# Transposing on TensorE in place of a round trip through DRAM, in the last five of 64 graphs

## The chip, the cores and the metric

The kernel runs on one core of a Trainium2 chip. The metric is the device time of one execution in microseconds (us). The names of the engines in the profile are PE (TensorE, matrix products and transposes by product), PEld (its loading of weights), DVE (VectorE), ACT (ScalarE), POOL (GpSimd) and SP (SyncE, which issues most transfers).

## The reference, cut to what matters

Each of 64 independent graphs has 256 nodes with 256 features (`x`) and a 256 x 256 integer adjacency (`adj`). Four layers follow each other, each with a residual and a layer norm around it:

```python
def _layernorm(x, axis=-1, eps=1e-5): ...           # no scale, no shift
x = _layernorm(x + _L0_gnn_ref(x, adj, ...))        # 8-head masked attention and a feed-forward of 1024
x = _layernorm(x + _L1_gnn_ref(x, adj, ...))        # graph attention (GAT)
x = _layernorm(x + _L2_gnn_ref(x, adj, ...))        # graph attention, then elu
x = _layernorm(x + _L3_gnn_ref(x, adj, ...))        # two relational convolutions, each with elu

# a graph attention (layers 1 and 2)
hidden = x @ W                                      # 256 x 256
e = leaky_relu(f_i[:, None] + f_j[None, :], 0.2)    # f_i, f_j: hidden times two vectors
out = softmax(where(adj > 0, e, -big)) @ hidden

# a convolution (twice in layer 3); with these inputs one of the two relations is empty
out = x @ w_root + b
for r in range(R):
    out = out + (einsum('ij,id->jd', masks[r], x) / deg[r]) @ w_rel[r]
h = elu(out)
```

Everything is in 32-bit floating point. [...] the input `x` of `x @ W`, which lies with nodes on partitions, must first be turned so that features lie on partitions. This happens five times in each graph after the projections: once ahead of the feed-forward, and once ahead of each of the two graph attentions and the two convolutions.

## The kernel before

A planner records every operation of every graph with a cost, and a list scheduler then fixes the order in which each engine executes them. Several graphs are in flight at a time. The last five graphs (`LAST = 5`) have due times close together, so that they are worked on side by side. Buffers come from rings; the numbers are their sizes:

```python
RINGS = {..., "T": 4, ..., "turned": 1, "xT": 2}
DRAM = {"rows": 6}
...
plan.ring("bank", 8, bank)               # PSUM: eight banks

class Plan:
    PERIOD = 46.0
    LAST, SPACE = 5, 0.1
    def schedule(self):
        last = max(o.graph for o in self.ops) - self.LAST
        for i, o in reversed(list(enumerate(self.ops))):
            due = (min(o.graph, last) + self.SPACE * max(0, o.graph - last)) * self.PERIOD
            ...
```

There are two ways to turn a tile `xt` of 256 nodes by 256 features. The first is used ahead of the feed-forward: four transposes on TensorE into one PSUM bank, and one copy out of it on ScalarE.

```python
def transposed(xt):
    xT, pt = new("T", [P, KB, N]), new("bank", [P, KB, N])
    def issue():
        for kb in range(KB):
            for i in range(NB):
                nc.tensor.transpose(pt()[:, kb, i * P : (i + 1) * P], xt()[:, i, kb * P : (kb + 1) * P], ident)
    pe("full", 0.44, issue, [xt], [pt], [xT])
    act(0.47, lambda: nc.scalar.copy(xT(), pt()), [pt], [xT])
    return xT
```

The second, called a bounce here, is used ahead of graph attentions and convolutions. VectorE transposes blocks of 32 x 32 into `turned`, four transfers store it in DRAM (`rows`), and one transfer loads it back with the blocks in place:

```python
def bounced(xt):
    turned, rows, xT = new("turned", [P, 4, NB * KB, 32]), new("rows", [P, NB * KB, 4, 32]), new("T", [P, NB * KB, P])
    dve(0.63, lambda: nc.vector.transpose(turned()..., xt()...), [xt], [turned], "uses")
    for a in range(4):
        op("SP", 0.5, lambda a=a: nc.sync.dma_start(rows()...[:, :, a, :], turned()[32 * a : 32 * a + 32]...),
           [turned], [(rows, a)], lag=SENT)
    op("SP", 0.5, lambda: nc.sync.dma_start(xT()..., rows()...), [rows], [xT], lag=BACK)
    return xT, lambda kb, i: xT()[:, KB * i + kb, :]
```

A bounce puts the features of a group of 128 on the partitions in another order: feature 32 b + c lies on partition 4 c + b. The rows of the weights of graph attentions and convolutions are loaded in that order once, at the start (`spread`), so that the product is the same.

The two users, cut to the steps that follow each other. A graph attention:

```python
def gat(xt, layer, gm, seen, bias, finish):
    xT, xT_at = bounced(xt)
    ...
    # per half: product with w (PE), copy of the result to h (ACT or DVE)
    # spread of one column over the partitions (PE), e = min(. + ., gm) (DVE), leaky relu (DVE), exp (ACT)
    # per half: product of e with h (PE), reciprocal and residual (DVE, in layer 2 also an exp on ACT)
    # then layer_norm: statistics (DVE), root (POOL), apply (ACT)
```

A convolution:

```python
def conv(h, layer, rel, rdeg):
    hT, hT_at = bounced(h)
    # per half: product with w, 512 columns (PE), hi = rounded part (ACT), lo = rest (DVE), o = . + bias (DVE)
    # per half: gather by rel (PE), o = o + . * rdeg (DVE)
    act(0.52, lambda: nc.scalar.activation(n(), o(), AF.Exp), [o], [n])
    act(0.52, lambda: nc.scalar.activation(n(), n(), AF.Identity, bias=minus[:, 0:1]), [n], [n])
    dve(0.60, lambda: nc.vector.scalar_tensor_tensor(o(), n(), 0.0, o(), op0=ALU.min, op1=ALU.max), [n, o], [o], "uses")
    return o
```

Of the kernel before, what the change touches and what calls it, by code (L numbers as in the profile page):

```python
# [17 lines left out]
P = 128  # L18
# [2 lines left out]
BIG = 1e30  # L21
NO_EDGE = -346.0


SENT, BACK = 3.0, 4.5

# [186 lines left out]
def tile_gnn_stack(ctx: ExitStack, tc: tile.TileContext, t: dict, out: bass.AP):  # L213
# [16 lines left out]
    nc = tc.nc  # L230
    x_in, adj_in = t["x"], t["adj"]
    B, N, D = x_in.shape
    assert N == 2 * P and D == 2 * P and B % 2 == 0
    G = B // 2
    KB = D // P
# [250 lines left out]
    def main_path(plan):  # L486
# [86 lines left out]
        def graph(g):  # L573
# [9 lines left out]
            def act(cost, issue, reads, writes):  # L583
                op("ACT", cost, issue, reads, writes)
# [4 lines left out]
            def tok(ring, dtype=F32):  # L589
                return new(ring, [P, NB, D], dtype)  # L590
# [20 lines left out]
            def transposed(xt):  # L611
# [9 lines left out]
                act(0.47, lambda: nc.scalar.copy(xT(), pt()), [pt], [xT])  # L621
                return xT

            def bounced(xt):

                turned, rows, xT = new("turned", [P, 4, NB * KB, 32]), new("rows", [P, NB * KB, 4, 32]), new("T", [P, NB * KB, P])
                dve(0.63, lambda: nc.vector.transpose(turned().rearrange("p b q n -> p (b q n)"),  # L629
                                                      xt().rearrange("p i (k b c) -> p b (i k) c", k=KB, b=4)),  # L630
                    [xt], [turned], "uses")
                for a in range(4):
                    op("SP", 0.5, lambda a=a: nc.sync.dma_start(  # L633
                        rows().rearrange("(c b) q a n -> c (b q) a n", b=4)[:, :, a, :],
                        turned()[32 * a : 32 * a + 32].rearrange("c b q n -> c (b q) n")), [turned], [(rows, a)], lag=SENT)
                op("SP", 0.5, lambda: nc.sync.dma_start(xT().rearrange("p q n -> p (q n)"), rows().rearrange("p q a n -> p (q a n)")),
                   [rows], [xT], lag=BACK)
                return xT, lambda kb, i: xT()[:, KB * i + kb, :]
# [178 lines left out]
                return y  # L817

            def gat(xt, layer, gm, seen, bias, finish):
                xT, xT_at = bounced(xt)  # L820
                w, c_w = gw[layer], c_gw[layer]
                h, e, z = new("h", [P, NB, HW]), tok("e"), tok("X")
                for i in range(NB):
                    ph = new("bank", [P, D + 2])
                    pe("full", 0.87, lambda i=i, ph=ph: product(ph(), lambda kb: xT_at(kb, i),
                                                                lambda kb: w[:, kb, :], KB), [xT, c_w], [ph], [h])
                    if bias is None:
                        act(0.27, lambda i=i, ph=ph: nc.scalar.copy(h()[:, i, 0 : D + 2], ph()), [ph], [(h, i)])
                    else:
                        dve(0.34, lambda i=i, ph=ph: nc.vector.tensor_tensor(h()[:, i, 0 : D + 2], ph(), bias, op=ALU.add),  # L830
                            [ph], [(h, i)])
                dve(0.07, lambda: nc.vector.memset(h()[:, :, ONE : ONE + 1], 1.0), [(h, 0), (h, 1)], [(h, "one")])
                dve(0.07, lambda: nc.vector.tensor_tensor(seen_fg[:, seen], h()[:, :, F_COL : G_COL + 1],
                                                          h()[:, :, F_COL : G_COL + 1], op=ALU.mult), [(h, 0), (h, 1)], [], "uses")
                pf = new("bank", [P, N])

                def spread():
                    for i in range(NB):
                        nc.tensor.transpose(pf()[:, i * P : (i + 1) * P],  # L839
                                            h()[:, i, F_COL : F_COL + 1].to_broadcast([P, P]), ident)  # L840

                pe("full", 0.22, spread, [(h, 0), (h, 1)], [pf], [e])
                for i in range(NB):
                    dve(0.40, lambda i=i: nc.vector.scalar_tensor_tensor(e()[:, i, :], pf(), h()[:, i, G_COL : G_COL + 1],  # L844
                                                                         gm()[:, i, :], op0=ALU.add, op1=ALU.min),
                        [pf, (h, i), gm], [(e, i)])
                dve(0.60, lambda: nc.vector.scalar_tensor_tensor(e(), e(), SLOPE, e(), op0=ALU.mult, op1=ALU.max), [e], [e],
                    "uses")
                act(0.52, lambda: nc.scalar.activation(e(), e(), AF.Exp), [e], [e])  # L849
                for i in range(NB):  # L850
                    po, r = new("bank", [P, HW]), new("r", [P, 1])
                    pe("full", 0.87, lambda i=i, po=po: product(po(), lambda kt: e()[:, kt, i * P : (i + 1) * P],
                                                                lambda kt: h()[:, kt, :], NB), [e, h], [po], [z, r])
                    dve(0.08, lambda po=po, r=r: nc.vector.reciprocal(r(), po()[:, ONE : ONE + 1]), [po], [r])
                    finish(i, z, po, r)
                return z
# [37 lines left out]
            def conv(h, layer, rel, rdeg):  # L894

                w, c_w, bias = conv_w[layer], c_cw[layer], conv_b[layer]
                hT, hT_at = bounced(h)
                o, hi, lo, n = tok("o"), new("hi", [P, NB, D + 2], F32R), tok("lo", F32R), tok("e")  # L900
                cols = D if layer else D + 2
                for i in range(NB):
                    po = new("bank", [P, 2 * D])
                    pe("full", 1.72, lambda i=i, po=po: product(po(), lambda kb: hT_at(kb, i),
                                                                lambda kb: w[:, kb, :], KB), [hT, c_w], [po], [hi, lo, o])
                    act(0.27, lambda i=i, po=po: nc.scalar.copy(hi()[:, i, 0:D], po()[:, D:]), [po], [(hi, i)])  # L906
                    dve(0.34, lambda i=i, po=po: nc.vector.tensor_tensor(
                        lo()[:, i, :], po()[:, D:], hi()[:, i, 0:D].bitcast(F32), op=ALU.subtract), [po, (hi, i)], [(lo, i)])
                    dve(0.33, lambda i=i, po=po: nc.vector.tensor_tensor(o()[:, i, :], po()[:, 0:D], bias, op=ALU.add),
                        [po], [(o, i)])  # L910
                if layer == 0:
                    dve(0.07, lambda: nc.vector.memset(hi()[:, :, D:].bitcast(F32), 1.0), [(hi, 0), (hi, 1)], [(hi, "ones")])
                for j in range(NB):
                    pa = new("bank", [P, D + 2])
                    terms = [(0, hi, cols), (0, lo, D), (1, lo, D), (1, hi, cols)]

                    def gather(j=j, pa=pa):
                        for c, (i, part, n) in enumerate(terms):
                            nc.tensor.matmul(pa()[:, 0:n], lhsT=rel()[:, i, j * P : (j + 1) * P], rhs=part()[:, i, 0:n],  # L919
                                             start=(c == 0), stop=(c == len(terms) - 1))  # L920

                    pe("full", 0.48, gather, [rel, hi, lo], [pa])
                    if layer == 0:
                        def inverse(j=j, pa=pa):
                            nc.vector.tensor_scalar(rdeg()[:, j : j + 1], pa()[:, D : D + 1], 1.0, None, op0=ALU.max)
                            nc.vector.reciprocal(rdeg()[:, j : j + 1], rdeg()[:, j : j + 1])

                        dve(0.25, inverse, [pa], [(rdeg, j)])
                    dve(0.40, lambda j=j, pa=pa: nc.vector.scalar_tensor_tensor(  # L929
                        o()[:, j, :], pa()[:, 0:D], rdeg()[:, j : j + 1], o()[:, j, :], op0=ALU.mult, op1=ALU.add),  # L930
                        [pa, (rdeg, j), (o, j)], [(o, j)])

                act(0.52, lambda: nc.scalar.activation(n(), o(), AF.Exp), [o], [n])
                act(0.52, lambda: nc.scalar.activation(n(), n(), AF.Identity, bias=minus[:, 0:1]), [n], [n])
                dve(0.60, lambda: nc.vector.scalar_tensor_tensor(o(), n(), 0.0, o(), op0=ALU.min, op1=ALU.max),
                    [n, o], [o], "uses")
                return o

            xT = input_transposed()
            adj = load("adj", adj_graph[g], I32)  # L940
            am, gm = masks(adj)
            xt = load("x", x_graph[g], F32)
# [4 lines left out]
            xt = feed_forward(x1, load("xr", x_graph[g], F32))  # L947
            xt = layer1(xt, gm)
            xt = layer2(xt, gm)
            rel = relation(load("adj", adj_graph[g], I32))  # L950
            rdeg = new("rdeg", [P, NB])
            h = conv(conv(xt, 0, rel, rdeg), 1, rel, rdeg)
# [270 lines left out]
```

## Time and profile before

The time is 2896.01 us, the median of three runs (2893.25 to 2898.55). The profiled execution has a span of 2897.1 us with a mean granted TensorE clock of 0.991. What matters in it:

| | |
|---|---|
| bounces in the program | 256 (four in each of 64 graphs) |
| VectorE block transposes for them (`turned<-X`, `turned<-o`) | 192 and 64 instructions, 134.9 and 45.0 us busy |
| stores into `rows` | 1024 of 64 KB, 2.2 us to landing |
| loads out of `rows` | 256 of 256 KB, 2.8 us to landing |
| transposes on TensorE ahead of the feed-forward (`bank<-ident,X`) | 256, 39.9 us busy |
| copies of those out of their bank on ScalarE (`T<-bank`) | 64, 37.5 us busy |

The page of a profile gives the busy time of each engine, then the span in 40 equal slices with a digit for each (9 means 90% busy or more), the transfers, and the chain of work that ended last, followed back from the last instruction. A row of a group of instructions names line, engine, operation, what is written and read, their shapes and count, then the busy time and the mean duration in ns of one, then the idle time of the engine just ahead of them and what ended it. A busy engine on its own says little: what a change is worth in a stretch of time is read from what the next operation of that stretch waited for.

### The profile page before, as it was taken

The page shows a single profiled execution, that of the slowest core. Times are in us where ns is not written, and L with a number is a line of the kernel's source. Part 1 is how long each engine was busy: PE and PEld are TensorE (multiplying, and loading weights), DVE is VectorE, ACT ScalarE, POOL GpSimd, SP SyncE. Part 2 cuts the span into 40 slices and gives each one's busy share as a digit, 9 for nine tenths or more (in the row PEclk, how much of TensorE's full clock was granted, in tenths as well). Part 3 has the DMA queues.
Part 4 walks back from the last instruction along what each step waited for, and adds up shares of the span by engine and source line. Part 5 has one row for each costly group of instructions (what it writes and reads, how often), then busy time and mean ns, then how long its engine had stood idle before and what let it go on. Part 6 is the DMA issues. An engine that isn't in the chain of part 4 may idle for free.

```text
span 2897.1 us, 50588 instructions
## 1 busy us (share of the span) xinstructions
PE 2805.3 (97%) x16182; PEld 2128.1 (73%) x16182; DVE 2523.0 (87%) x6557; ACT 1540.4 (53%) x3713; POOL 789.1 (27%) x1685
## 2 busy tenths in 40 slices
PE   8999999999999999999999999999999999999975
PEld 6776777777777767777777777777777777777853
DVE  6879899989989898999889898899888998999686
ACT  3555555546455555655555465555555655555343
POOL 2232223222223222222222322232231332222221
PEclk9999999999999999999999999999999999999998
DMA  7454455445444444454444544444444544443342
GB/s 183 81 108 88 99 101 102 89 101 102 95 92 100 87 94 94 98 101 93 104 97 93 98 99 99 100 91 102 86 93 96 109 88 93 105 90 72 67 83 70
DMA packets 844512, 278.32 MB, mean 96 GB/s; under 512 B 692656, under 2 KB 810672, under 8 KB 844240
## 3 DMA queue, kind: packets, MB, share of 16 engines
q1 hardware_dynamic: 808800, 240.27, 37.7%
q0 software_dynamic: 35440, 34.76, 8.5%
q8 instruction: 131, 2.15, 0.3%
q14 instruction: 141, 1.16, 0.1%
HBM read 157.43 MB, written 83.89 MB: 83 GB/s over the span
## 4 chain that ended last, share of the span: by engine, by line
PE 82%; DVE 10%; ACT 3%; DMA 2%; issue 2%; POOL 1%; SPq 1%; DVEq 0%; POOLq 0%; ACTq 0%
PE bank L657 67%; PE bank L919 4%; PE bank L776 3%; PE bank L751 3%; PE bank L771 2%; DMA rows<-turned 2%; DVE p L759 1%; PE bank L618 1%; DVE turned L629 1%; PE bank L839 1%; SPq L633 1%; DVE st L666 1%; DVE o L929 1%; DVE both L763 1%; DVE e L844 1%
## 5 line engine op out<-in xcount | busy, mean ns | idle before, releaser
L671 POOL TENSOR_SCALAR rstd<-mv 128x2 f32<-128x2 f32 x384 | 104.4, 272 | 1869.8 <-DVE mv L668 1496.7
L678 ACT ACTIVATE X<-X,rstd 128x256 f32<-128x256 f32 x640 | 349.8, 597 | 244.7 <-POOL rstd L674 230.1
L657 PE MATMUL bank<-cw,T 128*128 128x512 f32 x1024 | 467.9, 600 | 9.6 <-DMA T<-rows 9.1
L657 PE MATMUL bank<-T,w 128*128 128x256 f32 x2048 | 471.6, 380 | 5.2 <-ACT p L757 2.6
L657 PE MATMUL bank<-w,hid 128*128 128x256 f32 x2048 | 460.1, 380 | 0.0
L657 PEld LDWEIGHTS bank<-w,hid 128*128 128x128 f32 x2048 | 385.9, 190 | 62.7 <-issue 10.4
L657 PEld LDWEIGHTS bank<-T,w 128*128 128x128 f32 x2048 | 382.7, 190 | 64.5 <-issue 6.9
L757 ACT ACTIVATE p<-bank 128x512 f32<-128x512 f32 x512 | 299.9, 598 | 87.8 <-PE bank L751 87.6
L657 PEld LDWEIGHTS bank<-cw,T 128*128 128x128 f32 x1024 | 192.2, 192 | 209.3 <-issue 195.2
L759 DVE TENSOR_TENSOR p<-p,am 128x512 f32<-128x512 f32 x512 | 332.8, 680 | 10.8 <-ACT p L757 10.7
L672 POOL TENSOR_TENSOR rstd<-rstd,neghalf 128x2 f32<-128x2 f32 x384 | 305.7, 796 | 32.1
L809 ACT ACTIVATE hid<-bank,col_b 128x256 f32<-128x256 f32 x512 | 209.4, 474 | 113.8 <-PE bank L657 112.1
L657 PE MATMUL bank<-xT,wqkv 128*128 128x256 f32 x1024 | 251.6, 387 | 13.4 <-DVE xT L650 12.9
L657 PE MATMUL bank<-h,e 128*128 128x259 f32 x1024 | 253.8, 388 | 11.0 <-ACT e L849 9.3
L657 PE MATMUL bank<-gw,T 128*128 128x258 f32 x1024 | 249.1, 384 | 2.1 <-ACT inv L783 1.5
L657 PEld LDWEIGHTS bank<-h,e 128*128 128x128 f32 x1024 | 192.7, 192 | 66.6 <-issue 19.3
L666 DVE BATCH_NORM_STATS2 st<-X 128x6 f32<-128x256 f32 x640 | 237.5, 413 | 1.8
L906 ACT CAST hi<-bank 128x256 fp32r<-128x256 f32 x256 | 94.6, 370 | 263.4 <-PE bank L657 262.6
L657 PEld LDWEIGHTS bank<-xT,wqkv 128*128 128x128 f32 x1024 | 189.7, 192 | 54.0 <-issue 13.5
L780 DVE RECIPROCAL inv<-bank 128x256 f32<-128x256 f32 x128 | 220.0, 1734 | 8.8 <-PE bank L776 8.6
L657 PEld LDWEIGHTS bank<-gw,T 128*128 128x128 f32 x1024 | 191.1, 191 | 36.7 <-issue 5.2
L629 DVE STREAM_TRANSPOSE turned<-X 128x512 f32<-128x512 f32 x192 | 134.9, 703 | 45.0 <-DMA rows<-turned 23.0
(121 smaller groups left out, 4775.4 us busy)
## 6 DMA issues: line engine op xcount, KB each, us to landing
rows<-turned SPq DMA_DIRECT2D x1024, 64.0 KB, 2.2
T<-rows SPq DMA_DIRECT2D x256, 256.0 KB, 2.8
adj<-in_adj_dram SPq DMA_DIRECT2D x128, 256.0 KB, 3.0
blocks<-in_x_dram SPq DMA_DIRECT2D x512, 32.0 KB, 2.3
x<-in_x_dram SPq DMA_DIRECT2D x64, 256.0 KB, 3.0
xr<-in_x_dram SPq DMA_DIRECT2D x64, 256.0 KB, 2.8
xr<-row_ln_b POOLq DMA_DIRECT2D x64, 256.0 KB, 4.4
x<-row_bo POOLq DMA_DIRECT2D x64, 256.0 KB, 4.8
```

What stands on the lines that cost most here:

```text
L629: dve(0.63, lambda: nc.vector.transpose(turned().rearrange("p b q n -> p (b q n)"), xt().rearrange("p i (k b c) -> p b (i k) c", k=KB, b=4 ...
L657: nc.tensor.matmul(dst, lhsT=lhs(c), rhs=rhs(c), start=(c == 0), stop=(c == n - 1))
L666: nc.vector.bn_stats(stat()[:, i, :], y()[:, i, :])
L671: nc.gpsimd.tensor_scalar(rstd()[:, 0, :], mv()[:, :, 1], 1.0, EPS, op0=ALU.mult, op1=ALU.add)
L672: nc.gpsimd.tensor_tensor(rstd()[:, 0, :], rstd()[:, 0, :], neghalf[:, 0:NB], op=ALU.pow)
L678: nc.scalar.activation(y()[:, i, :], y()[:, i, :], AF.Identity, bias=rstd()[:, 1, i : i + 1], scale=rstd()[:, 0, i : i + 1])
L757: act(0.58, lambda pr=pr, k=k, sr=s[r]: nc.scalar.activation(pr(), sr(), AF.Exp, accum_out=seen_sum[:, k : k + 1]), [s[r]], [pr])
L759: dve(0.60, lambda pr=pr, kt=kt: nc.vector.tensor_tensor(pr(), pr(), am()[:, kt, None, :].to_broadcast([P, KB, N]), op=ALU.mult), [pr, am] ...
L780: dve(1.62, lambda hg=hg, pc=pc: nc.vector.reciprocal(inv()[:, hg, :], pc()[:, 1, :]), [pc], [(inv, hg)])
L809: act(0.36, lambda f=f, k=k, ph=ph: nc.scalar.activation(hid()[:, f + k, :], ph()[:, k, :], AF.Relu, bias=b1[:, f + k : f + k + 1]), [ph, ...
L906: act(0.27, lambda i=i, po=po: nc.scalar.copy(hi()[:, i, 0:D], po()[:, D:]), [po], [(hi, i)])
L919: nc.tensor.matmul(pa()[:, 0:n], lhsT=rel()[:, i, j * P : (j + 1) * P], rhs=part()[:, i, 0:n], start=(c == 0), stop=(c == len(terms) - 1))
```

## The change: TensorE transposes behind a spreading copy

In the last five graphs the four bounces of each graph are replaced by the first way, with a copy on ScalarE ahead of it. The copy writes the features of each group of 128 in the order in which the weights' rows lie (feature 32 b + c to column 4 c + b), so the transposed tile has on its partitions what a bounce would have put there, and the weights stay as they are. The purpose is to shorten the way from a tile to its transpose at the end of the program. In the other 59 graphs bounces stay. The copy's buffer comes from the same ring, `turned`, that has one buffer.

```diff
+QUICK = 5
...
+            def rearranged(xt):
+
+                if g < B - QUICK:
+                    return bounced(xt)
+                spread = tok("turned")
+                act(0.8, lambda: nc.scalar.copy(spread().rearrange("p i (k c b) -> p (i k) c b", k=KB, b=4),
+                                                xt().rearrange("p i (k b c) -> p (i k) c b", k=KB, b=4)), [xt], [spread])
+                xT = transposed(spread)
+                return xT, lambda kb, i: xT()[:, kb, i * P : (i + 1) * P]
+
             def bounced(xt):
...
             def gat(xt, layer, gm, seen, bias, finish):
-                xT, xT_at = bounced(xt)
+                xT, xT_at = rearranged(xt)
...
-                hT, hT_at = bounced(h)
+                hT, hT_at = rearranged(h)
```

## The prediction

> **What bounds the kernel now.** I read the page first: the engine totals and the 40 slices. TensorE has work for nearly all of the span, and only the first slice and the last two are not full.
>
> ```profile
> PE 2805.3 (97%) x16182; PEld 2128.1 (73%) x16182; DVE 2523.0 (87%) x6557; ACT 1540.4 (53%) x3713; POOL 789.1 (27%) x1685
> PE   8999999999999999999999999999999999999975
> ```
>
> The reader should take from it a ceiling: 2897.1 - 2805.3 = 91.8 us of TensorE idle in all, and the change acts only in the last five of 64 graphs, that is at the right-hand end of the second line. So I next asked for the busy time by stretches over that end.
>
> ```profile
> 2725.00:2737.00 12.00, 12.00 (x59) 10.48 (x58) 7.86 (x24) 5.72 (x13) 3.71 (x12) 1.00 0.16 44
> 2737.00:2760.00 23.00, 17.86 (x81) 14.20 (x79) 18.52 (x63) 7.77 (x16) 9.08 (x22) 1.00 0.51 91
> 2760.00:2800.00 40.00, 31.79 (x116) 22.88 (x117) 31.27 (x102) 17.58 (x38) 7.40 (x20) 0.87 0.38 76
> 2800.00:2830.00 30.00, 24.77 (x91) 14.58 (x90) 25.11 (x80) 12.38 (x26) 4.13 (x12) 1.00 0.45 91
> 2830.00:2860.00 30.00, 21.58 (x64) 11.05 (x63) 23.00 (x70) 11.96 (x25) 4.69 (x12) 0.89 0.43 94
> 2860.00:2884.80 24.80, 15.92 (x49) 7.95 (x47) 13.61 (x39) 8.26 (x16) 2.57 (x8) 0.86 0.22 59
> 2884.80:2897.10 12.30, 0.19 (x2) 0.09 (x2) 2.98 (x9) 2.45 (x4) 1.28 (x4) 0.61 0.09 27
> ```
>
> The columns are the stretch, its length, then busy time of PE, weight loads, DVE, ACT and POOL with their instructions, the granted clock, the DMA share and GB/s. TensorE is full until 2737. From there to its last matmul at 2884.8 it works 17.86 + 31.79 + 24.77 + 21.58 + 15.92 = 111.9 of 147.8 us, so **35.9 us are idle**. The last 12.3 us are the end of the last layer norm and the output's transfer, where TensorE has nothing to do. Up to 2737 there is no free TensorE time to win by a shorter wait.
>
> In the tail no engine is full: VectorE, summed likewise, works 111.5 of the 147.8 us and ScalarE 58.0. So work there is bound by the chain from one operation to the next. I looked at the DMA queue's timeline and the chain that ended last:
>
> ```profile
> 2808.95 2.56 SPq L633 DMA_DIRECT2D rows<-turned  x4
> 2813.17 0.33 SPq L636 DMA_DIRECT2D T<-rows  x1
> 2814.79 2.56 SPq L633 DMA_DIRECT2D rows<-turned  x4
> ```
>
> ```profile
> 2843.55 0.62 DVE turned L629
> ...
> 2846.13 2.23 DMA rows<-turned
> 2848.43 4.25 DMA T<-rows
> 2852.81 5.38 PE bank L657 x8
> ...
> 2870.06 0.62 DVE turned L629
> ...
> 2872.65 2.21 DMA rows<-turned
> 2875.00 2.59 DMA T<-rows
> 2877.73 5.09 PE bank L657 x8
> ```
>
> Two things are to be seen. A bounce (VectorE block transpose, four stores to DRAM, one load back) takes 2877.73 - 2870.06 = 7.7 us on the chain when nothing delays it, and 2852.81 - 2843.55 = 9.3 us the time before. And the bounces stand one behind the other: 19 are issued from 2737.41 to 2855.85, one each 118.4 / 18 = 6.6 us, while one holds the only `turned` buffer for about 0.7 (transpose) + 4.3 (first store issued to the last landed, 2808.95 to 2813.17) = 5 us. That single buffer is taken some three quarters of the time in the tail.
>
> [...] the spreading copy reads with a step of 32 elements, and no instruction in this trace shows what ScalarE pays for that.
>
> **The change part by part.** Five graphs have four bounces each, so 20 of the 256 are replaced. The rows that price it:
>
> ```profile
> L629 DVE STREAM_TRANSPOSE turned<-X 128x512 f32<-128x512 f32 x192 | 134.9, 703 | 45.0 <-DMA rows<-turned 23.0
> L621 ACT COPY T<-bank 128x512 f32<-128x512 f32 x64 | 37.5, 588 | 40.7 <-PE bank L618 40.3
> L849 ACT ACTIVATE e<-e 128x512 f32<-128x512 f32 x128 | 80.8, 631 | 113.6 <-DVE e L847 107.3 <-DVE h L832 3.4 <-DVE r L854 2.5
> ```
>
> Removed: 20 x 0.703 = 14.1 us of VectorE, 80 stores and 20 loads, the 20 turns on the DMA path. Added on TensorE: four transposes per turn. Where they ran back to back ahead of the feed-forward the chain shows 0.44 us for four, so 20 x 0.44 = 8.8 us. Added on ScalarE: the copy out of the bank, 0.588 us, and the spreading copy. The kernel's own table plans 0.8 for it where it plans 0.52 for the exp that takes 0.631, so I scale: 0.8 x 0.631 / 0.52 = 0.97 us, an estimate. Together 20 x 1.56 = 31 us.
>
> Moved: the instruction order is made by the kernel's list scheduler. Comparing the orders of both programs, every engine's list is the same up to about 86% of TensorE's instructions, and from there graphs near the end are interleaved differently, with the same work. TensorE is full in that region, so I count nothing for it before 2737.
>
> Latency of one turn on the path: 0.97 + 0.44 + 0.59 us of work and three hand-overs of about 0.15 us (the chain's gap between the bank's arrival and the next engine's start) = 2.4 us, against 7.7 to 9.3. A turn on the path saves **5.3 to 6.9 us**. The last graph alone has two complete ones on the last 54 us of the chain, which is 11 to 13 us if nothing else steps in.
>
> The ceiling: with TensorE never idle from 2737 to its last matmul the stretch would be 111.9 + 8.8 = 120.7 us in place of 147.8, 27 us less, so about 2869. It won't reach that. Five graphs go through the same four stages; each stage waits on VectorE and ScalarE several times, and towards the end fewer graphs are left to fill gaps. TensorE is at 111.9 / 147.8 = 76% there now. I choose 92% for after: 120.7 / 0.92 = 131 us, a gain of 16.6 us. At 85% the gain is 5.8 us, at 97% it is 23 us. VectorE would then have 97 us and ScalarE 89 us of work in 131, so neither is a bound by itself. Sum: 2896 - 16 = **2880 us**.
>
> **The rivals.** (a) *ScalarE's place in the chain.* [...] its load in the tail grows from 58 to 89 us, and a spreading copy that waits for its layer norm holds up exp and evictions of other graphs behind it. For it: the chain already passes ScalarE five times per convolution. Against: it is idle 60% of the tail. If it took half of the gain the time would be 2888. (b) *The saved latency is hidden anyway.* With five graphs in flight, another graph's matmuls fill a bounce, and only the last graph's bounces count. For it: TensorE is 76% busy in spite of the bounces, and the trace puts only 9.4 us of direct TensorE waiting from 2737 on the loads from DRAM. The gain would be the 11 to 13 us of the last graph less the 8.8 us of added TensorE work where that lies on the path: 2884 to 2893. (c) *TensorE becomes the bound*, as the single buffer no longer paces the graphs and VectorE loses 14 us: 2869 to 2872. (d) *Banks.* Each new turn takes one of eight PSUM banks for about a microsecond; the tail has no attention scores, which take four at once, so I expect no loss.
>
> **Range and chances.** The time lies between the ceiling of (c) and a little short of nothing gained; (b) and (a) pull up from the middle. I take 2868 to 2892. Faster by over 2% needs 58 us, more than the tail's whole idle time; slower by over 2% needs more than all of the added work on both engines, laid end to end. Both get 0.01.
>
> **What would show it right or wrong.** In the changed profile TensorE should still be full until about 2735; the DMA queue should issue no stores into `rows` after the last old graph; the chain of the last 150 us should have no transfers but the output's; the spreading copy should show as a ScalarE row of 20 near 0.9 us. TensorE's busy time should rise by about 9 us in total or somewhat less, and its share between the last full stretch and its last matmul should be near 92%. A spreading copy of 1.5 us or more, or TensorE idle behind ScalarE in the tail, would make me too optimistic; a tail that stays full to within 20 us of the end, too cautious. If the order changed before the tail opened gaps there, the prediction fails for a reason outside its sum.

## The result, and the profile after

The changed kernel takes 2878.34 us (median of four runs, 2875.3 to 2882.61), the kernel before in the same series 2897.01 us. The ratio is 0.9939 with a 95% interval of 0.9921 to 0.9956: 18 us saved, where 16 were forecast. The engine totals and the first row of the 40 slices of the changed kernel's page:

```profile
PE 2803.4 (98%) x16262; PEld 2133.7 (74%) x16262; DVE 2507.6 (87%) x6537; ACT 1568.3 (55%) x3753; POOL 786.5 (27%) x1685
PE   7999999999999999999999999999999999999987
```

TensorE executes 80 more matrix instructions than before and yet is busy 1.9 us less. VectorE falls by 15.4 us and ScalarE rises by 27.9 us. The end is where the gain lies, as the busy times by stretches of the changed kernel show (columns as before: stretch, length, PE, weight loads, DVE, ACT, POOL, clock, DMA share, GB/s; the last stretches are cut at this kernel's own last matmul and end):

```profile
2725.00:2737.00 12.00, 12.00 (x58) 10.48 (x58) 3.77 (x13) 5.50 (x12) 3.75 (x9) 1.00 0.22 44
2737.00:2760.00 23.00, 17.61 (x79) 14.15 (x79) 16.65 (x55) 11.53 (x20) 7.37 (x20) 0.93 0.12 24
2760.00:2800.00 40.00, 36.58 (x174) 28.05 (x172) 33.28 (x120) 27.57 (x54) 8.62 (x24) 1.00 0.07 14
2800.00:2830.00 30.00, 27.41 (x115) 17.71 (x115) 25.54 (x88) 21.90 (x41) 5.63 (x15) 1.00 0.09 20
2830.00:2862.00 32.00, 27.67 (x107) 15.76 (x106) 26.53 (x82) 22.57 (x42) 6.02 (x15) 1.00 0.09 32
2862.00:2875.20 13.20, 0.73 (x7) 0.41 (x5) 3.52 (x10) 3.42 (x6) 1.66 (x6) 0.66 0.14 45
```

TensorE is full up to 2737 as before, and its last real work ends near 2862 in place of 2884.8. Between, it works 17.61 + 36.58 + 27.41 + 27.67 = 109.3 of 125 us, or 87%. TensorE's idle time there fell from 35.9 to 15.7 us. Direct waits for loads of `rows` were only 9.4 us of it before, so about half of what went had stood behind something else: direct waits for VectorE fell from 16.1 to 4.5 us, those for ScalarE went from 10.2 to 11.2. The largest hole left lies in the first of these stretches, which has 5.4 us of idle time in all. In the three stretches after it the granted clock is 1.00; before the change it was 0.86 to 0.89 in three stretches.

A turn on the last chain is short now. First the last product of a convolution before, then the last transposes and that product after, from TensorE's timelines (start, length, engine, line, operation, count, and in brackets the idle time ahead and what ended it):

```profile
2877.73 5.08 PE L657 MATMUL bank<-cw,T 128*128 128x512 f32 x8 [5.71 <-DMA T<-rows]
```

```profile
2855.12 0.66 PE L620 MATMUL bank<-ident,turned 128*128 128x128 f32 x4
2856.93 3.70 PE L669 MATMUL bank<-cw,T 128*128 128x512 f32 x8 [1.16 <-ACT T L623]
```

The idle time ahead of the product fell from 5.71 to 1.16 us, and the same eight matrix instructions took 3.70 us in place of 5.08. The spreading copies, from the tile view of `turned` (shortest, median, longest in ns, first and last start):

```profile
L631 ACT COPY turned<-X x15: 1064/1107/1120, 2690.0 to 2833.4; 128x512 f32<-128x512 f32 x15
L631 ACT COPY turned<-o x5: 1082/1095/1134, 2807.5 to 2853.9; 128x512 f32<-128x512 f32 x5
```

From the start of the last copy to its product is 2856.93 - 2853.9 = 3.0 us, against 7.7 before.

### The profile page after: what moved, and what is told of

Its sections match the earlier page's. It is cut to its first block, busy times and chain, and to the rows that moved or that the text cites. A ratio compares the mean times of both kernels' runs of the same rounds, so it can differ in the third digit from the quotient of the medians.

```text
span 2875.2 us, 50600 instructions
## 1 busy us (share of the span) xinstructions
PE 2803.4 (98%) x16262; PEld 2133.7 (74%) x16262; DVE 2507.6 (87%) x6537; ACT 1568.3 (55%) x3753; POOL 786.5 (27%) x1685
## 3 DMA queue, kind: packets, MB, share of 16 engines
q1 hardware_dynamic: 763680, 229.77, 35.9%
## 4 chain that ended last, share of the span: by engine, by line
PE 85%; DVE 7%; ACT 3%; DMA 2%; issue 2%; POOL 1%; SPq 0%; DVEq 0%; POOLq 0%; ACTq 0%
PE bank L669 70%; PE bank L931 4%; PE bank L763 4%; PE bank L788 3%; PE bank L783 2%; PE bank L620 1%; PE bank L851 1%; DVE p L771 1%; DMA rows<-turned 1%; ACT X L690 1%; DVE st L678 1%; ACT p L769 1%; DVE o L941 1%; DVE turned L641 0%; DVE both L775 0%
## 5 line engine op out<-in xcount | busy, mean ns | idle before, releaser
L775 DVE TENSOR_TENSOR both<-p 128x512 f32<-128x512 f32 x256 | 167.0, 679 | 0.0
```

The costliest lines, as they stand in the source:

```text
L775: dve(0.60, lambda r=r: nc.vector.tensor_tensor(both[r](), p[0, r](), p[1, r](), op=ALU.add), [p[0, r], p[1, r]], [both[r]], "uses")
```

## The experiments

The diffs are against the changed kernel. The ratios are to the kernel before on the same chip. A second measure leaves out what differs from run to run early in the program. It is the time, in each profile, from the start of the four transposes ahead of the eighth-last feed-forward (near 2476 us; TensorE's order is the same in these kernels up to there) to the end, and is called the **remainder**. It comes from one execution of each kernel and its own spread was not measured, so one or two microseconds of it say little. For the last two rows with ten graphs the order differs earlier, so none is given.

| kernel | ratio (95% interval) | remainder, us | less than before |
|---|---|---|---|
| before | | 420.8 | |
| changed | 0.9939 (0.9921 to 0.9956) | 399.5 | 21.3 |
| bounces, with the added work unused beside them | 1.0011 (1.0005 to 1.0018) | 422.8 | -2.0 |
| bounces, two buffers for the last five graphs | 0.9960 (0.9948 to 0.9972) | 407.4 | 13.4 |
| last graph alone | 0.9953 (0.9942 to 0.9965) | 407.6 | 13.2 |
| the four ahead of the last | 0.9972 (0.9962 to 0.9983) | 411.5 | 9.3 |
| last graph, and two buffers for the other four | 0.9922 (0.9908 to 0.9935) | 400.5 | 20.3 |
| changed, copy not spreading | 0.9925 (0.9911 to 0.9938) | 398.4 | 22.4 |
| changed, copy into a ring of its own | 0.9900 (0.9885 to 0.9915) | 392.0 | 28.8 |
| changed, copy into a ring of twelve | 0.9913 (0.9899 to 0.9926) | 391.2 | 29.6 |
| changed, no copy for graph attentions | 0.9880 (0.9865 to 0.9895) | 389.2 | 31.6 |
| the same, other copies into the ring of twelve | 0.9874 (0.9859 to 0.9889) | 389.0 | 31.8 |
| ten graphs, shared ring | 0.9940 (0.9927 to 0.9953) | | |
| ten graphs, ring of twelve | 0.9928 (0.9915 to 0.9942) | | |

**The work without the latency.** The last 20 bounces stay, and the new operations are executed beside them into buffers that nobody reads.

```diff
                 if g < B - QUICK:
                     return bounced(xt)
-                spread = tok("turned")
+                spread = tok("dead")
...                                         # the copy, the transposes, the copy out of the bank into "deadT"
-                return xT, lambda kb, i: xT()[:, kb, i * P : (i + 1) * P]
+                return bounced(xt)
```

> Bounces stay everywhere; beside each of the 20 last ones the spreading copy, the four TensorE transposes and the copy out of the bank are executed as well, into buffers nobody reads. So the added work is there and the saved latency is not. Theory (the latency of a turn fills TensorE's idle time in the tail): no gain, 0 to 9 us slower than the kernel before, 2896 to 2905. Rival (the list scheduler merely found a luckier order once something was different): 2875 to 2890 would speak for it.

It was 0.11% slower, 3 us. So the added 9 us of TensorE and some 30 us of ScalarE work lie for the most part in time that was idle, and a different program alone, without the shorter turn, gains nothing. That speaks against a chance of the scheduler.

**A second buffer for the bounces.**

```diff
-RINGS = {..., "turned": 1, ...}
+RINGS = {..., "turned": 1, "turnedB": 2, ...}
...
+                return bounced(xt)             # in rearranged, for all graphs
...
-                turned, ... = new("turned", [P, 4, NB * KB, 32]), ...
+                turned, ... = new("turnedB" if g >= B - QUICK else "turned", [P, 4, NB * KB, 32]), ...
```

> Bounces stay everywhere; the last five graphs have a ring of two buffers of their own for the block transposes, so that bounces can overlap. Theory (latency of one turn): a small gain, up to 5 us, 2891 to 2896. Rival (the single buffer paces the graphs in the tail): most of the 18 us, 2878 to 2884.

It gained 0.40%, 12 us, at the lower end of what the rival expected: two thirds of what the change gained, with every turn still a bounce. This ring also keeps the bounces of the last five graphs apart from older ones. The DMA queue's timeline of this run shows bounces issued two at a time:

```profile
2755.62 5.24 SPq L644 DMA_DIRECT2D rows<-turnedB  x8
...
2788.26 5.25 SPq L644 DMA_DIRECT2D rows<-turnedB  x8
...
2800.78 5.25 SPq L644 DMA_DIRECT2D rows<-turnedB  x8
```

What it leaves is the latency of the last bounces. Its last product in TensorE's timeline waits as before and then runs slowly:

```profile
2863.14 6.61 PE L668 MATMUL bank<-cw,T 128*128 128x512 f32 x8 [4.15 <-DMA T<-rows]
```

**The last graph alone, and the four ahead of it.**

```diff
-QUICK = 5
+QUICK = 1
```

> Only the very last graph takes the new way. Rival (with five graphs in flight a bounce is hidden behind other graphs, and only the last graph's own chain counts): about all of the gain, 11 to 18 us, 2878 to 2885. Theory (every turn of the five opens gaps on TensorE): a fifth to two fifths of it, 2889 to 2892.

```diff
-                if g < B - QUICK:
+                if g < B - QUICK or g == B - 1:
```

> The complement of the run with the last graph alone: four of the last five graphs take the new way, the very last keeps its four bounces. Its bounces then never wait for the single buffer. If the last graph's own chain is what counts: a small gain, 2890 to 2896 where before is 2896. If the single buffer's pacing is what counts: as much as the second buffer gave, about 12 us, 2884. If every turn opens gaps on TensorE in proportion: four fifths of 18, 2882.

The first met its rival's expectation (its ratio makes 2882 of 2896), the second, 2888, none of its three. The last graph alone saved 13.2 us of the remainder and the other four together 9.3; the sum, 22.5, is about the 21.3 of all five. A turn of the last graph is worth several times one of the others. But each of these runs also takes bounces away from the single buffer, so neither tells the last chain from the buffer.

**The last graph and a second buffer together.**

```diff
+RINGS = {..., "turned": 1, "turnedB": 2, ...}
...
-                if g < B - QUICK:
+                if g < B - 1:
...                                         # bounces of the other four use turnedB
```

> The last graph takes the new way and the other four keep bounces with two buffers. Each alone gave 12 to 14 us, and the whole change 18. If the two are the same thing seen twice (the last graph's chain): no more than the last graph alone, 2882 where before is 2896. If they add until TensorE's work in the tail is the floor: all of the change's 18 us or a little more, 2876 to 2879, as the 31 us of ScalarE work and 8.8 us of TensorE work are mostly saved.

The ratio is 0.9922 (2873 of 2896, a little better than either expectation) and the remainder 20.3 us shorter, as good as the whole change with 16 of its 20 turns still bounced. The two do not add (13.2 + 13.4 would be 26.6), and neither is the other seen twice. That so few new turns reach the same end suggests that something in the changed kernel gave part of its gain away.

**The copy without its stride.** Here the copy takes the columns in their order, so that the last five graphs are not computed as the reference asks.

```diff
-act(0.8, lambda: nc.scalar.copy(spread().rearrange("p i (k c b) -> p (i k) c b", k=KB, b=4),
-                                xt().rearrange("p i (k b c) -> p (i k) c b", k=KB, b=4)), [xt], [spread])
+act(0.8, lambda: nc.scalar.copy(spread(), xt()), [xt], [spread])
```

> The changed kernel with the ScalarE copy reading its columns one after the other. It leaves out the reordering, so that the last five graphs multiply columns by the wrong weight rows; the work is otherwise the same. The copy should fall from 1.10 to about 0.6 us. Theory (latency of a turn on the last chain): 4 x 0.5 = 2 us below the changed kernel. Rival (ScalarE's order holds up the tail): up to 20 x 0.5 = 10 us below it.

```profile
L631 ACT COPY turned<-X x15: 602/620/639, 2691.4 to 2833.4; 128x512 f32<-128x512 f32 x15
```

The copy takes 0.62 us, so reading with a step of 32 elements cost 1.11 - 0.62 = 0.49 us. Ten microseconds less of ScalarE work shortened the remainder by 1.1 us; by the ratios it is 4 us, with overlapping intervals. The 10 us of the rival are not seen: with the shared ring, ScalarE's time isn't what chiefly holds up the tail.

**No copy for the graph attentions.** A second copy of their weights with rows in natural order is loaded at the start, and the tiles of the last five graphs are transposed directly. Everything is computed.

```diff
+                if natural:                    # asked for by gat, not by conv
+                    xT = transposed(xt)
+                    return xT, lambda kb, i: xT()[:, kb, i * P : (i + 1) * P]
                 spread = tok("turned")
...
-                w, c_w = gw[layer], c_gw[layer]
+                w, c_w = (gw[layer], c_gw[layer]) if g < B - QUICK else (gw_n[layer], c_gwn[layer])
```

> The changed kernel, but the two graph attentions of the last five graphs use a second copy of their weights with rows in natural order, so that their tiles are transposed on TensorE directly and ten of the twenty ScalarE copies fall away. Everything is computed. Theory: 2 x 1.1 us on the last graph's chain and 11 us less of ScalarE work beside it: 2 to 5 us below the changed kernel, if the added weight loads at the start cost nothing. Rival (TensorE's work is the floor): the same as the changed kernel within 1 us.

The ratio is 0.9880, so it gained far more than either expectation: 10.3 us of remainder beyond the changed kernel (17 us by the ratios). After the run above, the time of ten copies is unlikely to be the whole of that. The changed kernel's largest hole, at 2746 to 2750, shows another cause. In its DMA queue's timeline, a bounce of an older graph holds `turned`:

```profile
2743.23 2.57 SPq L645 DMA_DIRECT2D rows<-turned  x4
2747.49 0.34 SPq L648 DMA_DIRECT2D T<-rows  x1
```

The stores have landed when the load is issued, at 2747.49. The next copy starts at 2748.41, behind a layer norm that ScalarE's order has ahead of it, with TensorE idle behind the copy:

```profile
2747.41 1.09 ACT L690 ACTIVATE X<-X,rstd 128x256 f32<-128x256 f32 x2 [2.15 <-POOL rstd L686]
2748.41 1.06 ACT L631 COPY turned<-X 128x512 f32<-128x512 f32 x1
...
2749.53 0.66 PE L620 MATMUL bank<-ident,turned 128*128 128x128 f32 x4 [3.60 <-ACT turned L631]
```

The planner gives out the rings' buffers while it fixes the order, so the one buffer shows in the order: the copy is put behind the bounce, and here behind the layer norm too. Three such old bounces stand in this tail. At the second one the copy waits for the stores themselves:

```profile
2778.73 1.08 ACT L631 COPY turned<-X 128x512 f32<-128x512 f32 x1 [1.86 <-DMA rows<-turned]
```

The copies and the bounces share one buffer, so a copy that needs it for 2 us in the tail comes after a bounce that holds it for 5. Where TensorE is full a copy holds it longer: the first one starts at 2690.0 us, and the first transposes of a copied tile at 2715.5.

**A ring of its own, and a ring of twelve.**

```diff
-                spread = tok("turned")
+                spread = tok("spread")         # a new ring of one buffer
```

> The changed kernel, but the spreading copy writes into a ring of its own with one buffer, so that it no longer waits for bounces of older graphs that hold the shared single buffer, nor they for it. If that sharing is what the direct transposes of the graph attentions got rid of: 8 to 15 us below the changed kernel, ratio to before 0.989 to 0.991. If it was the copy's own latency and ScalarE time: within 3 us of the changed kernel, 0.993 to 0.995.

```diff
-                spread = tok("turned")
+                spread = tok("p")              # the attention's ring of twelve
```

> The same with many buffers: the spreading copy takes one of the twelve buffers of the attention's ring, which is idle in the tail. If the sharing with bounces is the cause: the same as with one buffer of its own, within 3 us. If the depth of the ring is (two turns cannot overlap): below it by 3 us or more.

One buffer apart from the bounces shortens the remainder by 7.5 us beyond the changed kernel, twelve by 8.3 (11 and 8 us by the ratios). So the sharing is the cause of most of the 10.3 us, and more depth than one buffer of its own adds nothing clear. A shared ring of two buffers was not run, so keeping apart isn't told from having one buffer more in all. With a ring of its own, the same place has two copies start while the older graph's bounce is under way:

```profile
2749.56 1.10 ACT L631 COPY spread<-X 128x512 f32<-128x512 f32 x1
2750.20 2.57 SPq L645 DMA_DIRECT2D rows<-turned  x4
2752.67 1.11 ACT L631 COPY spread<-X 128x512 f32<-128x512 f32 x1
2754.45 0.34 SPq L648 DMA_DIRECT2D T<-rows  x1
```

TensorE's direct waits for the copy from 2737 on, first in the changed kernel, then with its own ring (total us, times, longest):

```profile
PE bank L620 <- ACT turned L631: 6.5, 5, 3.6
```

```profile
PE bank L620 <- ACT spread L631: 3.3, 3, 1.8
```

**Both together.** Direct transposes for the graph attentions, and the other copies in the ring of twelve.

> Direct transposes for the graph attentions and, for the convolutions, a spreading copy into the attention's ring. If the ring was the cause of the whole gain of the direct transposes: the same as the run with many buffers and no more than that. If both count: 2 to 6 us below the direct transposes with the shared ring, ratio 0.986 to 0.988.

The edits are those above. It takes 2863.93 us, a ratio of 0.9874, the lowest of all, but not to be told from the 0.9880 of direct transposes with the shared ring. With the graph attentions off the ring, little seems to be left of the sharing. What leaving the copies out is worth beyond the ring of twelve stays open. The remainder has 2.2 us (31.8 against 29.6), but in this profile the last product was slow:

```profile
2845.28 6.75 PE L679 MATMUL bank<-cw,T 128*128 128x512 f32 x8 [1.17 <-ACT T L630]
```

In the changed kernel it took 3.70 us, 3.05 less. The times differ by more, 0.9874 against 0.9913 with intervals that do not overlap: about 11 us.

**Ten graphs.** `QUICK = 10`, first with the shared ring, then with the ring of twelve.

> The last ten graphs take the new way; the five added ones are largely worked on where TensorE is full. Theory: there the latency is hidden and only the added TensorE work counts, up to 20 x 0.44 = 8.8 us above the changed kernel, 2880 to 2888. Rival (a shorter turn, or 14 us less of VectorE, helps everywhere): at or below the changed kernel, 2865 to 2878.

> The last ten graphs take the new way with the spreading copy in the attention's ring. The run with ten graphs and the shared ring came out like the changed kernel with five, but there two things were mixed: more TensorE work, and fewer old bounces beside the tail. With the ring out of the way only the work is left. If turns where TensorE is full cost their 0.44 us each: 20 x 0.44 = 8.8 us above the run with five graphs and many buffers, ratio 0.994 to 0.995. If they cost nothing there: the same ratio as that run, 0.990 to 0.992.

The first came out like five graphs (0.9940 against 0.9939), but it also keeps old bounces further from the tail. The second is 0.9928 against 0.9913 with five, about 4 us more, half the expected 8.8, and the two intervals overlap. TensorE's busy time rose by 2809.5 - 2799.8 = 9.7 us. Whether a turn costs its full 0.44 us where TensorE is full stays open; no gain is seen there.

## Why the prediction was right, and where it wasn't

**Where the gain lies: right.** TensorE is full to 2737 in both profiles and nearly the whole difference comes after. The reordering ahead of the tail left no trace.

**The turn: right in kind, short in size.** Forecast 2.4 us, measured 3.0. On the last turn the spreading copy, put at 0.97 us, took 1.1, and the four transposes, put at 0.44, took 0.66; after them the copy out of the bank stood about 0.5 us behind another graph's layer norm on ScalarE. The hand-overs, put at 0.15 us each, took 0.06 us from the copy to the transposes and 0.05 from the copy out of the bank to the product; on the chain before, 0.02 us lie between the last product's end and the next engine, and the 0.14 stand after a load's landing. The 0.97 had been scaled, by the planner's table, from an exp of as many elements that took 631 ns. The copy in order took 620 ns, close to that exp, and the step added the 0.49 us; what ScalarE does in that time no run shows.

**TensorE's work in the tail: wrong by 11 us.** The sum took 111.9 us before as fixed, added 8.8 for the transposes and had 120.7. It measured 109.3. Part of the busy time before was the same work done more slowly, at a lower granted clock. The 96 matrix instructions of the convolutions after 2737, in the windows of the kernel before and of the changed one (stretch, length, PE busy, weight loads, clock, DMA share, GB/s):

```profile
2737.00:2900.00 163.00, 48.02 (x96) 19.24 (x96) 0.89 0.37 77
```

```profile
2737.00:2900.00 163.00, 43.15 (x96) 17.66 (x96) 0.96 0.08 20
```

The same work is 4.9 us shorter. The eight matrix instructions of one product show it at closer range. In the kernel before (columns: stretch, length, PE, weight loads, DVE, ACT, POOL, clock, DMA share, GB/s):

```profile
2852.81:2858.19 5.38, 5.38 (x10) 2.36 (x10) 3.67 (x12) 1.36 (x3) 1.56 (x4) 0.68 0.48 96
2859.92:2863.52 3.60, 3.60 (x10) 1.33 (x8) 2.11 (x5) 1.61 (x3) 0.00 (x0) 1.00 0.42 120
2877.73:2882.81 5.08, 5.08 (x10) 2.33 (x10) 0.76 (x2) 1.47 (x3) 0.28 (x2) 0.72 0.15 52
```

(Two instructions of the neighbours reach into each window.) The first and the last of these products stood behind waits of 3.05 and 5.71 us for a load and took 5.38 and 5.08 us at a granted clock of 0.68 and 0.72; the one between them, with no wait ahead, took 3.60 at 1.00. After the change the last product, behind a gap of 1.16, took 3.70 at 1.00. As many instructions took less time also where bounces stay: with two buffers for them, TensorE's 399 instructions after 2737 were busy 108.5 us, and as many in the kernel before 112.1, though its last product took 6.61 us behind a gap of 4.15. The gap just ahead doesn't decide alone: in the kernel with both changes (direct transposes and the ring of twelve) the eight took 6.75 us after only 1.17, with another gap of 1.09 us shortly before, at a granted clock of 0.50 from 2845 to 2850 (0.86 over the stretch from 2830 to 2854.2). What lowers the clock in these places was not shown. Of the other 6.5 us of the difference, 3.5 lie in the graph attentions' product with `e` and in the gathers by `rel`, which have as many instructions in both and took 24.8, 15.2 and 11.5 us before and 23.1, 14.7 and 10.2 after. The rest was not taken apart; the graphs' interleaving at 2737 isn't quite the same in both.

**TensorE's share: wrong the other way.** 92% was chosen, 87% measured. The two misses nearly cancel: 120.7 / 0.92 = 131 us forecast, 109.3 / 0.87 = 125 us measured. The figure of 2880 came out close partly by that.

**The ceiling of 2869: wrong.** Two kernels went below it (2865.95 and 2863.93 us), for the first reason: it took 120.7 us of TensorE work as left after 2737, and in the lowest kernel that work measured 110.2.

**The rivals.** (a), ScalarE's order, did not take half of the gain: 10 us less of its work moved the remainder by 1 us. What leaving copies out gains beyond the ring, which stays open, may be in part ScalarE's time. (b), only the last graph counts, holds in part: it has more than its share, but the other four are worth 9 us. The prediction itself misread the chain here. It gave both bounces on the last 54 us to the last graph, but after the product at 2852.81 the chain passes, at 2862.79, the residual sum that ends a graph, so that bounce belonged to another one. (c) had the right thing in it and stopped short. The single buffer did pace the tail: freeing it alone gave 13.4 us of 21.3. But the prediction said the buffer would no longer pace the graphs, and it still did, since the copies queue in the same ring behind old bounces; a ring of its own would have brought 28.8. That was to be read in the diff (`tok("turned")`) beside the ring's size. From two-buffered bounces (13.4) to unshared short turns (29.6) the remainder falls by 16.2 us. That is an estimate of the worth of the shorter turn itself, if two buffers are enough for the bounces; more were not tried. (d), banks, was not tried by itself.

**What would show it.** The forecast that the chain of the last 150 us would have no transfers but the output's, and no stores once the old graphs are done, holds but for the three old bounces inside the tail, which I hadn't placed there. TensorE did stand idle behind ScalarE, named as a sign of too much optimism: 6.5 us for the spreading copies and 3.9 for the copies out of the bank. TensorE's total, forecast to rise by up to 9 us, fell by 1.9.

## What to carry to other kernels

Where several units of work are in flight and still no engine is full, count how long each ring's buffer is held per use: the single buffer here, held for 5 us at a time, paced a tail in which no engine was full, and a second one alone took 13.4 us off the remainder. When a quick operation replaces a slow one, don't let it share a ring with the slow ones that stay. And look at the granted clock before taking the busy time of a gappy stretch as the work left over: here the last product took 5.08 us at a clock of 0.72 behind a wait of 5.71 us, and 3.70 at 1.00 behind one of 1.16, and the sum made from that busy time was 11 us above what was measured (120.7 against 109.3).

## What the runs showed of the hardware that was not expected

A ScalarE copy of 128 x 512 elements of four bytes took 1.11 us in the changed kernel, where it read with a step of 32 elements, and 0.62 us in the run where it read in order (medians of 15). Eight matrix instructions of 512 columns took 3.70 us after TensorE had been idle for 1.16 (changed kernel), 5.08 after 5.71 (before) and 6.61 after 4.15 (two buffers), and in the kernel with direct transposes and the ring of twelve 6.75 after 1.17, so the gap just ahead didn't tell how slow they would be. Two such groups at a granted clock of 1.00 took 3.60 (before) and 3.70 us (changed kernel), one at 0.72 took 5.08 and one at 0.68 5.38 (both before). And 30 us of ScalarE and 9 us of TensorE work added to a tail of some 150 us, in which TensorE had been idle for 36 us, cost 3 us (the run with the added work unused).
